# Attention products in quarters of 64 rows by 64 columns, with a second bank for half of the keys

## The chip, the cores and the metric

The kernel runs on one core of a Trainium2 chip. The metric is the device time of one execution in microseconds (us): the median of several runs. A core has five engines that run their own instruction queues in order: TensorE (PE in the profile, its weight loads shown apart as PEld), VectorE (DVE), ScalarE (ACT), GpSimd (POOL) and SyncE (SP, which here only issues DMAs). TensorE's results land in PSUM tiles, of 512 fp32 columns in up to 128 partitions here, called banks below.

## The reference

Two layers over 2708 tokens of 256 channels. Only the attention of the first layer is touched by the change. It has four query heads and two key/value heads of 64 channels, so each key/value head serves two query heads, and it is causal:

```python
q = (h @ wq.T).reshape(Bx, Tx, NH, HD).transpose(0, 2, 1, 3)     # NH = 4, HD = 64
k = (h @ wk.T).reshape(Bx, Tx, NKV, HD).transpose(0, 2, 1, 3)    # NKV = 2
v = (h @ wv.T).reshape(Bx, Tx, NKV, HD).transpose(0, 2, 1, 3)
...
scores = jnp.einsum('bhtd,bhsd->bhts', q, k) / jnp.sqrt(jnp.float32(HD))
scores = jnp.where(causal[None, None], scores, jnp.float32(-1e+30))
att = jax.nn.softmax(scores, axis=-1)
y = jnp.einsum('bhts,bhsd->bhtd', att, v).transpose(0, 2, 1, 3).reshape(Bx, Tx, Cx)
x = x + y @ wo.T
```

Before it comes a graph layer whose softmax is decided by the largest adjacency value of each row; after it comes a mixture of eight experts with two chosen per token (router, gated up and down products). The second layer repeats graph layer and experts with other weights, without attention. All is fp32.

## The kernel before

**Stages.** `first` does the graph part and the attention of layer 0, then come the experts of layer 0 (`experts_blocks`), the graph part of layer 1 (`second`) and the experts of layer 1. The change is all in `first`, which takes the first 470 us or so. Tokens lie in 22 tiles of 128 (the last has 20 rows).

**What runs in `first`.** For each tile, `tile_in` loads the adjacency row block, finds the largest value and its index on DVE (`top`, L994, and `index`, L998), fetches the chosen row by an indirect DMA (`fetch`, L1016), makes q, k and v (L1046) and turns q and k (L1069). For each pair of tiles, `pair(t0)` with t0 = 0, 2, ..., 20 does the attention of those 256 queries against all keys up to them, one block of 128 keys after the other. For a block `sb`:

- `scores` (L1120): for each key/value head g one product of 64 rows (the channels of the head, partitions 64g to 64g + 63) by 128 columns (the keys), streaming 512 columns (two query tiles of two heads). The two g's use the upper and the lower half of the rows of the array and run at the same time. The result is the PSUM tile `stt`, one bank for each g, in two buffers.
- `exps` (L1126): ACT takes the exponential of both banks into the SBUF tile `e`, of which there are four.
- `mask` (L1135): POOL clears what lies above the diagonal, only in the last two blocks.
- `values` (L1146), for two blocks at once: for each g one product of 128 rows (the keys) by 64 columns (the channels of v), which adds into partitions 64g to 64g + 63 of the single PSUM bank `o`. The two g's use the left and the right half of the columns and run at the same time.
- `sums` (L1160, L1165): DVE adds `e` up over the blocks in the single SBUF tile `es`, and so frees `e`.

In the first three pairs (`on_pe`, t0 < 6) the sums are made on PE instead, into the bank `zs` (L1153). When a pair is through, `leave` copies `o` to SBUF (ACT, L1187), `spread` (L1198) sums `es` over partitions by a product with ones, DVE takes the reciprocal (L1203, `turn_over`), POOL multiplies (L1207, `weigh`), PE projects (L1221) and DVE joins the residual (L1225). After the pairs t0 = 4, 10, 16, 18 and 20, `route` makes the router's decision for the tiles that are through: a transposition (L408), logits (L423, into a tile `pg` in the bank `zs`), the choice and the ranks on DVE (L437 to L487, with two products at L467 and L468) and scatters of the rows to the experts on POOL (L1829).

**PSUM.** The stage holds eight banks: two `st` buffers of two banks each, two `mm` banks, one bank `o` and one bank `zs`.

**Who sets the order.** Nothing is scheduled on the fly. Each step is given to `Plan` by `add(engine, length, run, needs, take, give, rank)`; `Plan.issue` plays the steps through with the lengths written there, takes the lowest rank among those that can start, and emits the instructions in that order. So an engine's queue is fixed at build time, and a step that waits holds up all that stands behind it in its queue. Where PE would be idle for over 1 us by the plan and the bank `zs` or `o` is free, `Plan.fill` puts in products that nobody reads (`nobody`, L1287).

**After the last pair.** `early_blocks` runs the first experts' blocks of 128 tokens (L561, L584) in the banks `st`, `zs` and `o` while the last tiles are routed; the experts' stage proper begins after the scatter of the last tiles.

Of the kernel before, what the change touches and what calls it, by code (L numbers as in the profile page):

```python
# [10 lines left out]
F32 = mybir.dt.float32  # L11
AF = mybir.ActivationFunctionType
ALU = mybir.AluOpType
# [4 lines left out]
PE, SP = mybir.EngineType.PE, mybir.EngineType.SP  # L18
PSUM = bass.MemoryType.PSUM

P = 128
# [6 lines left out]
NH, NKV, HD = 4, 2, 64  # L28
# [37 lines left out]
def rows(t):  # L66
    return min(P, N - t * P)
# [6 lines left out]
class Plan:  # L74
# [16 lines left out]
    def add(self, engine, length, run, needs=(), take=(), give=(), rank=0.0, lands=0.0):  # L91
        step = dict(engine=engine, length=length, run=run, needs=[n for n in needs if n is not None],
                    take=take, give=give, rank=rank, lands=lands, end=None)
        self.steps.append(step)
        return step
# [54 lines left out]
def adj_ffn_kernel(ctx, tc, x, adj, vecs, bias_rows, tab, w_gnn0, w_gnn1, wqkv, wo,  # L150
                   r0, r1, w1_0, w3_0, w2_0, w1_1, w3_1, w2_1, out):
    nc = tc.nc
# [655 lines left out]
    def first(X, XB, norms, tops, hd, mb, xs, acc, arena, load_weights):  # L808
# [9 lines left out]
        W2 = NREP * P  # L818
        NQK = (NH + NKV) * HD
        with ExitStack() as s:  # L820
# [5 lines left out]
            afp = s.enter_context(tc.tile_pool(name="afp", bufs=1, space=PSUM))  # L826
            abs_ = s.enter_context(tc.tile_pool(name="abs", bufs=2, space=PSUM))
            qT = ap.tile([P, NT, NREP, P], F32, name="qT")
            kT = ap.tile([P, N], F32, name="kT")
            V = ap.tile([P, NT, NKV * HD], F32, name="V")  # L830
# [4 lines left out]
            for g in range(NKV):  # L835
                for i in range(2):
                    q = 64 * i + 32 * g
# [12 lines left out]
            add = plan.add  # L850
# [3 lines left out]
            for a, b in ((0, 4), (4, NT - 1)):  # L854
                loads.append(add("SP", 0.5, lambda a=a, b=b: nc.sync.dma_start(
                    out=X[:, a:b, :], in_=x[a * P:b * P, :].rearrange("(t p) c -> p t c", p=P)),
                    rank=-9.0, lands=1.5 + 0.4 * (b - a)))
# [22 lines left out]
            a = add("SP", 1.2, load_wq, loads, take=["e"], rank=1.5, lands=3.0)  # L880
# [218 lines left out]
            def pair(t0):  # L1099
# [3 lines left out]
                v = {}  # L1103
                on_pe = t0 < PE_SUMS
                rank = t0 + 2.5
                ready = [made[t0][0], made[t0 + 1][0]]
                end = None

                def c0(sb):
                    return W2 if sb == t0 + 1 else 0  # L1110

                for n in range(0, t0 + 2, 2):
                    two = sbs[n:n + 2]

                    def scores(sb):
                        r = rows(sb)
                        v[sb, "st"] = st = abs_.tile([P, NKV, 2 * W2], F32, tag="st", name="stt")
                        for g in range(NKV):
                            a, b = g * HD, (g + 1) * HD
                            nc.tensor.matmul(st[:r, g, c0(sb):], kT[a:b, sb * P:sb * P + r],  # L1120
                                             qT[a:b, t0 + (sb == t0 + 1):t0 + 2, :, :], start=True, stop=True)

                    def exps(sb):
                        r = rows(sb)
                        v[sb] = e = abe.tile([P, NKV, 2 * W2], F32, tag="e", name="e")
                        nc.scalar.activation(e[:r, :, c0(sb):], v[sb, "st"][:r, :, c0(sb):], AF.Exp,  # L1126
                                             scale=1.0 / HD ** 0.5)

                    def mask(sb):
                        r, e = rows(sb), v[sb]  # L1130
                        if t0 == 0 and c0(sb):
                            nc.gpsimd.memset(e[:r, :, :c0(sb)], 0.0)
                        for g in range(NKV):
                            d = e[:r, g, c0(sb):c0(sb) + W2].rearrange("p (h c) -> p h c", h=NREP)
                            nc.gpsimd.affine_select(out=d, in_=d, compare_op=ALU.is_ge, fill=0.0, base=0,  # L1135
                                                    pattern=[[0, NREP], [1, P]], channel_multiplier=-1)

                    def values(n=n, two=two):
                        if n == 0:
                            v["o"] = afp.tile([P, 2 * W2], F32, tag="o", name="o")  # L1140
                            if on_pe:
                                v["zs"] = afp.tile([P, 2 * W2], F32, tag="zs", name="zs")
                        for i, sb in enumerate(two):
                            r, c = rows(sb), c0(sb)
                            for g in range(NKV):
                                nc.tensor.matmul(v["o"][g * HD:(g + 1) * HD, c:], V[:r, sb, g * HD:(g + 1) * HD],  # L1146
                                                 v[sb][:r, g, c:], start=(n + i == 0), stop=(n + i == t0 + 1))
                        if on_pe:
                            for i, sb in enumerate(two):
                                r, c = rows(sb), c0(sb) if t0 else 0  # L1150
                                for g in range(NKV):
                                    q = 64 * i + 32 * g
                                    nc.tensor.matmul(v["zs"][q:q + 32, c:], allones[:r, :32], v[sb][:r, g, c:],  # L1153
                                                     start=(n == 0), stop=(n == t0))

                    def sums(n=n, two=two):
                        a, b = two
                        if n == 0:
                            v["es"] = ab.tile([P, NKV, 2 * W2], F32, tag="es", name="es", bufs=1)
                            nc.vector.tensor_tensor(v["es"], v[a], v[b], ALU.add)  # L1160
                        else:
                            for sb in two:
                                r, c = rows(sb), c0(sb)
                                es = v["es"][:r, :, c:]
                                nc.vector.tensor_tensor(es, es, v[sb][:r, :, c:], ALU.add)  # L1165

                    es = []
                    for sb in two:
                        a = add("PE", 1.0, lambda f=scores, sb=sb: f(sb), ready, take=["st"], rank=rank)
                        scored[:] = [a]  # L1170
                        b = add("ACT", 1.0, lambda f=exps, sb=sb: f(sb), [a], take=["e"], give=["st"], rank=rank)
                        if sb >= t0:
                            b = add("POOL", 1.6, lambda f=mask, sb=sb: f(sb), [b], rank=rank)
                        es.append(b)
                    last = n == t0
                    if on_pe:
                        end = add("PE", 2.9, values, es + [end], take=["o", "zs"] if n == 0 else [],
                                  give=["e"] * 2, rank=rank)
                        ends = [end]
                    else:  # L1180
                        end = add("PE", 1.9, values, es + [end], take=["o"] if n == 0 else [], rank=rank)
                        ends = [add("DVE", 2.46 if n else 1.25, sums, es + [ends[0] if n else None, end],
                                    take=["es"] if n == 0 else [], give=["e"] * 2, rank=rank)]

                def leave():
                    v["ob"] = ab.tile([P, 2 * W2], F32, tag="osb", name="osb")
                    nc.scalar.copy(v["ob"], v["o"])  # L1187
                    if on_pe:
                        v["zb"] = ab.tile([P, NKV, 2 * W2], F32, tag="es", name="zsb", bufs=1)[:, 0, :]
                        nc.scalar.copy(v["zb"], v["zs"])  # L1190

# [13 lines left out]
                def weigh():  # L1205
                    y = v["yT"].rearrange("p t j c -> p (t j c)")
                    nc.gpsimd.tensor_tensor(out=y, in0=v["ob"], in1=y, op=ALU.mult)  # L1207

                a = add("ACT", 1.2 if on_pe else 0.6, leave, [end], take=["ob", "es"] if on_pe else ["ob"],
                        give=["o", "zs"] if on_pe else ["o"], rank=rank - 1)  # L1210
                a = add("PE", 0.9, spread, [a] + ends, take=["mm"], give=["es"], rank=rank - 1)
                a = add("DVE", 3.4, turn_over, [a], take=["yT"], give=["mm"], rank=rank - 1)
                a = add("POOL", 1.6, weigh, [a], give=["ob"], rank=rank - 1)
                for i in range(2):
                    t = t0 + i
                    r = rows(t)
# [16 lines left out]
                    b = add("PE", 0.9, project_out, [a], take=["mm"], give=["yT"] if i else [], rank=rank - 1)  # L1233
                    b = add("DVE", 0.45, join, [b, made[t][1]], give=["mm"], rank=rank - 1)
                    joined.append(b)
                    b = add("POOL", 1.1, sum_up, [b], rank=rank + 3)
# [2 lines left out]
                g0 = {4: 0, 10: 6, 16: 12, 18: 18, 20: 20}.get(t0)  # L1239
                if g0 is not None:  # L1240
                    sent[t0] = route(add, range(g0, t0 + 2), joined[g0:], summed[g0:] + [folded], cleared, 0, XB, xs[0], af, tr_tile,
                          "mm", lambda: afp.tile([P, 2 * W2], F32, tag="zs", name="pg"), "zs", rank + 3)

            for t in range(0, NT, 2):
                project(t)
# [15 lines left out]
            a = None  # L1261
            weights = []
            for e in range(2):
                a = add("SP", 6.0, lambda e=e: load_weights(e), cleared + [a], rank=NT + 3.0 + e, lands=3.0,
                        take=[] if e else [f"{a}{i}" for i in range(3) for a in ("adj", "low")])
# [1147 lines left out]
```

## Time and profile before

| | us |
|---|---|
| median of 3 runs | 1482.06 (1481.34 to 1487.33) |
| the profiled execution, its own time | 1481.93 |
| its span, first to last instruction | 1479.8 |
| PE busy | 1401.3 (95%) |
| DVE busy | 754.4 (51%) |
| ACT busy | 564.5 (38%) |
| POOL busy | 525.7 (36%) |
| `stt` products (L1120), busy | 132.4 |
| `o` products (L1146), busy | 124.3 |
| mean granted PE clock | 0.984 |

The profile is of one execution; 2.1 us of its time lie outside the span. "Busy" is the union of an engine's instructions in time. An fp32 product appears as two passes, each with its own weight load, so the 264 products at L1120 are 528 records of each kind. A shape such as 64\*128 64x512 is rows times columns of the weights in the array, then partitions and elements that stream. A releaser in brackets is what ended the idle time of the engine before that instruction.

### The profile page before, as it was taken

How to read it: one execution, taken by the hardware profiler on the slowest of the kernel's cores; microseconds unless marked ns; L12 is line 12 of the kernel's file. 1: busy time of each engine (PE TensorE's matmuls, PEld its weight loads, DVE VectorE, ACT ScalarE, POOL GpSimd, SP SyncE). 2: the span in 40 equal slices, each digit the busy share in tenths (PEclk: the TensorE clock that was granted, in tenths of full speed). 3: DMA queues.
4: the chain of work that ended last, by engine and by line, in shares of the span. 5: the costliest groups of instructions: out<-in, count | busy, mean ns of one | idle time of the engine just before them, and what ended most of it. 6: DMA issues, size and time to landing. Idle time of an engine off the chain costs nothing.

```text
span 1479.8 us, 20690 instructions
## 1 busy us (share of the span) xinstructions
PE 1401.3 (95%) x7344; PEld 1021.5 (69%) x7344; DVE 754.4 (51%) x1629; ACT 564.5 (38%) x1123; POOL 525.7 (36%) x677
## 2 busy tenths in 40 slices
PE   6878999999999999999999899999999999999995
PEld 5633433433334887888888878888768878888885
DVE  5688999975676322222222474767665322222221
ACT  2577866755544322222221454444333211222220
POOL 5677668773243312222222210031434212222222
PEclk9999999999999999999999999999999999999998
DMA  7689767440001476575212770624412867553111
GB/s 265 199 296 288 241 208 236 139 146 15 8 30 50 126 218 194 141 195 158 37 16 26 167 154 1 139 66 115 132 58 57 265 171 196 157 161 88 19 18 21
DMA packets 190679, 193.03 MB, mean 130 GB/s; under 512 B 90568, under 2 KB 162728, under 8 KB 187856
## 3 DMA queue, kind: packets, MB, share of 16 engines
q1 hardware_dynamic: 166262, 162.30, 35.5%
q0 software_dynamic: 20032, 25.71, 9.7%
q10 hardware_dynamic: 4270, 3.58, 0.7%
q8 instruction: 60, 0.98, 0.3%
q14 instruction: 55, 0.45, 0.1%
HBM read 119.81 MB, written 56.11 MB: 119 GB/s over the span
## 4 chain that ended last, share of the span: by engine, by line
PE 77%; DVE 8%; DMA 6%; POOL 4%; issue 2%; ACT 2%; another core or an unknown queue 0%; POOLq 0%; DVEq 0%; SPq 0%; ACTq 0%
PE pup L2085 23%; PE po L1602 14%; PE y L2100 12%; PE o L1146 5%; PE stt L1120 4%; DMA X<-hd,ix 3%; PE up L561 3%; PE pup L2116 3%; PE y L2150 1%; DVE es L1165 1%; DVE yT L1203 1%; PE pt L2063 1%; PE pm L1221 1%; PE po L948 1%; PE pt L584 1%
## 5 line engine op out<-in xcount | busy, mean ns | idle before, releaser
L2085 PE MATMUL pup<-xTs,arena 128*128 128x256 f32 (+2 forms) x1320 | 252.3, 350 | 0.6 <-ACT xTs L2068 0.6
L2085 PEld LDWEIGHTS pup<-xTs,arena 128*128 128x128 f32 (+1 forms) x1320 | 219.8, 190 | 27.7 <-PE y L2150 1.5
L1602 PE MATMUL po<-hb,PT 128*128 128x257 f32 (+2 forms) x968 | 226.0, 387 | 2.6 <-DVE PT L1595 2.6
L2089 ACT ACTIVATE sl<-pup 128x256 f32<-128x256 f32 (+1 forms) x210 | 73.7, 351 | 375.1 <-PE pup L2085 354.2
L1602 PEld LDWEIGHTS po<-hb,PT 128*128 128x128 f32 (+2 forms) x968 | 175.9, 188 | 41.6 <-issue 12.7
L2090 DVE TENSOR_TENSOR hT<-sl,pup 128x256 f32<-128x256 f32 (+1 forms) x210 | 79.6, 380 | 228.5 <-ACT sl L2089 228.3
L1126 ACT ACTIVATE e<-stt 128x1024 f32<-128x1024 f32 (+1 forms) x132 | 125.6, 986 | 93.0 <-PE stt L1120 63.8
L621 POOL DMA_INDIRECT out<-ys,XR x44 | 68.0, 1546 | 237.2 <-DVE ys L2103 169.2
L1165 DVE TENSOR_TENSOR es<-es,e 128x1024 f32<-128x1024 f32 x104 | 136.1, 1309 | 29.9 <-ACT e L1126 22.0
L621 POOL DMA_INDIRECT acc<-ys,XR x44 | 68.4, 1554 | 225.1 <-DVE ys L2103 153.7
L2100 PE MATMUL y<-arena,hT 128*128 128x256 f32 x612 | 136.7, 379 | 0.0
L1120 PE MATMUL stt<-qT,kT 64*128 64x512 f32 (+1 forms) x528 | 132.4, 611 | 4.3 <-ACT e L1126 3.9
L1829 POOL DMA_INDIRECT xs<-XR,place x88 | 93.3, 1061 | 91.7 <-DVE mk L1589 39.6
L1146 PE MATMUL o<-e,V 128*64 128x512 f32 (+1 forms) x528 | 124.3, 594 | 0.0
L2100 PEld LDWEIGHTS y<-arena,hT 128*128 128x128 f32 x612 | 114.3, 190 | 14.5
L1580 ACT ACTIVATE E<-sb,dcol 128x768 f32<-128x768 f32 (+1 forms) x88 | 75.3, 859 | 110.2 <-DVE PT L1595 106.7
L2103 DVE TENSOR_SCALAR ys<-y,XR 128x256 f32<-128x256 f32 x71 | 34.3, 484 | 146.6 <-PE y L2100 146.4
L2085 PE MATMUL pup<-xTs,room 128*128 128x256 f32 (+3 forms) x528 | 99.9, 346 | 0.0
L1120 PEld LDWEIGHTS stt<-qT,kT 64*128 64x128 f32 x528 | 44.4, 187 | 76.5 <-issue 62.3
L2085 PEld LDWEIGHTS pup<-xTs,room 128*128 128x128 f32 (+1 forms) x528 | 85.4, 189 | 9.8 <-PE y L2150 0.8
L1146 PEld LDWEIGHTS o<-e,V 128*64 128x64 f32 x528 | 33.0, 138 | 70.6 <-issue 55.6
L994 DVE MAX8 tops<-arena 128x8 f32<-128x2708 f32 (+1 forms) x22 | 65.3, 2970 | 0.3 <-DMA arena<-in_adj 0.3
(316 smaller groups left out, 1992.4 us busy)
## 6 DMA issues: line engine op xcount, KB each, us to landing
more<-in_w SPq DMA_DIRECT2D x48, 640.0 KB
arena<-in_adj SPq DMA_DIRECT2D x21, 1354.0 KB
arena<-in_w SPq DMA_DIRECT2D x36, 640.0 KB
mb<-mb SPq DMA_DIRECT2D x44, 352.0 KB
XR<-xs SPq DMA_DIRECT2D x80, 134.0 KB
xs<-none SPq DMA_DIRECT2D x16, 536.0 KB
room<-in_w SPq DMA_DIRECT2D x12, 640.0 KB
acc<-X SPq DMA_DIRECT2D x21, 128.0 KB
```

The lines of the kernel that those rows point to most:

```text
L621: i = nc.gpsimd.indirect_dma_start(out=acc[:, :], out_offset=bass.IndirectOffsetOnAxis(ap=tokens.bitcast(I32), axis=0), in_=ys, in_offset= ...
L1120: nc.tensor.matmul(st[:r, g, c0(sb):], kT[a:b, sb * P:sb * P + r], qT[a:b, t0 + (sb == t0 + 1):t0 + 2, :, :], start=True, stop=True)
L1126: nc.scalar.activation(e[:r, :, c0(sb):], v[sb, "st"][:r, :, c0(sb):], AF.Exp, scale=1.0 / HD ** 0.5)
L1146: nc.tensor.matmul(v["o"][g * HD:(g + 1) * HD, c:], V[:r, sb, g * HD:(g + 1) * HD], v[sb][:r, g, c:], start=(n + i == 0), stop=(n + i == t ...
L1165: nc.vector.tensor_tensor(es, es, v[sb][:r, :, c:], ALU.add)
L1580: nc.scalar.activation(e[:q, :n], sb[:q, i0:i1], AF.Exp, bias=dcol[:q, j:j + 1], scale=SLOPE - 1.0)
L1602: nc.tensor.matmul(v["po", i][:r, :F], v["PT", j][:q, a:a + r], hb[:q, j, :], start=(j == 0), stop=(j == NT - 1))
L1829: i = nc.gpsimd.indirect_dma_start(out=xs[:, :], out_offset=bass.IndirectOffsetOnAxis(ap=at, axis=0), in_=src, in_offset=None)
L2085: nc.tensor.matmul(pp[:to, i, :B, :], wn[:, c, :], xT[:, c, :B, :], start=(c == 0), stop=(c == KC - 1))
L2089: nc.scalar.activation(sl[:, :B, :], pp[:, 0, :B, :], AF.Silu)
L2090: nc.vector.tensor_tensor(hT[:, n, :B, :], sl[:, :B, :], pp[:, 1, :B, :], ALU.mult)
L2100: nc.tensor.matmul(y, hT[:, n, b, :], w[3][:, n, :], start=(n == 0), stop=(n == NHC - 1))
```

## The change

In the pairs from t0 = 6 on, each score product of 64 rows by 128 columns becomes two of 64 by 64 (keys 0 to 63 and 64 to 127 of the block), and each value product of 128 by 64 becomes two of 64 by 64. The second half of the keys of a value product adds into a bank of its own, `o2`, which takes the place of `zs`. The first three pairs stay as they were. `leave` moves from ACT to DVE in the pairs from t0 = 6 on: a copy of `o` and an addition of `o2`. `route` no longer has a bank for its logits; it uses the `mm` tile of its transposition, which so is held until ACT has copied the logits out (`keep`). The planned length of `values` goes from 1.9 to 1.75.

```diff
+                def keys(sb):
+                    r = rows(sb)
+                    return [(0, r)] if on_pe else [(p, min(p + HD, r)) for p in range(0, r, HD)]
...
                         for g in range(NKV):
                             a, b = g * HD, (g + 1) * HD
-                            nc.tensor.matmul(st[:r, g, c0(sb):], kT[a:b, sb * P:sb * P + r],
-                                             qT[a:b, t0 + (sb == t0 + 1):t0 + 2, :, :], start=True, stop=True)
+                            for p, q in keys(sb):
+                                nc.tensor.matmul(st[p:q, g, c0(sb):], kT[a:b, sb * P + p:sb * P + q],
+                                                 qT[a:b, t0 + (sb == t0 + 1):t0 + 2, :, :], start=True, stop=True)
...
+                            if not on_pe:
+                                v["o2"] = afp.tile([P, 2 * W2], F32, tag="zs", name="o2")
...
-                                nc.tensor.matmul(v["o"][g * HD:(g + 1) * HD, c:], V[:r, sb, g * HD:(g + 1) * HD],
-                                                 v[sb][:r, g, c:], start=(n + i == 0), stop=(n + i == t0 + 1))
+                                for p, q in keys(sb):
+                                    to = v["o2" if p else "o"]
+                                    nc.tensor.matmul(to[g * HD:(g + 1) * HD, c:], V[p:q, sb, g * HD:(g + 1) * HD],
+                                                     v[sb][p:q, g, c:], start=(n + i == 0), stop=(n + i == t0 + 1))
...
-                        end = add("PE", 1.9, values, es + [end], take=["o"] if n == 0 else [], rank=rank)
+                        end = add("PE", 1.75, values, es + [end], take=["o", "zs"] if n == 0 else [], rank=rank)
...
-                    nc.scalar.copy(v["ob"], v["o"])
-                    if on_pe:
+                    if not on_pe:
+                        nc.vector.tensor_copy(v["ob"], v["o"])
+                        nc.vector.tensor_tensor(v["ob"], v["ob"], v["o2"], ALU.add)
+                    else:
+                        nc.scalar.copy(v["ob"], v["o"])
...
-                a = add("ACT", 1.2 if on_pe else 0.6, leave, [end], take=["ob", "es"] if on_pe else ["ob"],
-                        give=["o", "zs"] if on_pe else ["o"], rank=rank - 1)
+                a = add("ACT" if on_pe else "DVE", 1.2, leave, [end], take=["ob", "es"] if on_pe else ["ob"],
+                        give=["o", "zs"], rank=rank - 1)
...
-                          "mm", lambda: afp.tile([P, 2 * W2], F32, tag="zs", name="pg"), "zs", rank + 3)
+                          "mm", None, "mm", rank + 3)
```

## The prediction

> **What bounds the kernel now.** The attention stage ends at about 474 us; what follows is untouched. I read first the forty slices of 37 us in the page, for where which engine is full:
>
> ```profile
> PE   6878999999999999999999899999999999999995
> ...
> DVE  5688999975676322222222474767665322222221
> ```
>
> DVE is at 9 only in slices 5 to 8 (148 to 296 us); PE is at 9 nearly everywhere. So I cut the stage at the starts of `spread` (L1198) and asked for busy times in each stretch. Columns: length, then busy us of PE, PEld, DVE, ACT and POOL with counts, the granted clock, the DMA share and rate:
>
> ```profile
> 252.40:290.00 37.60, 36.41 (x169) 15.93 (x169) 36.05 (x36) 26.47 (x45) 31.70 (x32) 0.95 0.55 168
> 290.00:339.00 49.00, 46.13 (x183) 16.98 (x185) 35.19 (x50) 26.39 (x48) 37.84 (x53) 0.97 0.40 133
> 339.00:379.40 40.40, 39.77 (x178) 14.01 (x176) 24.58 (x20) 21.12 (x33) 9.02 (x11) 1.00 0.02 8
> ```
>
> Two regimes. From 176 to 290 us (pairs 8 to 12) DVE is busy 109.8 of 114 us (36.55 + 37.22 + 36.05 over three stretches): it still finds maxima and indices of adjacency rows. From 290 us on (pairs 14 to 20) PE is the bound, and DVE has 13 to 16 us to spare in each stretch.
>
> Inside the second regime I read PE's weight loads in the timeline (start, us, engine, instruction, idle before it):
>
> ```profile
> 375.45 0.30 PEld L1120 LDWEIGHTS stt<-qT,kT 64*128 64x128 f32 x4 [0.81 <-issue]
> 375.99 0.19 PEld L1120 LDWEIGHTS stt<-qT,kT 64*128 64x128 f32 x2 [0.24 <-issue]
> 376.42 0.19 PEld L1120 LDWEIGHTS stt<-qT,kT 64*128 64x128 f32 x2 [0.23 <-issue]
> 377.37 0.20 PEld L1146 LDWEIGHTS o<-e,V 128*64 128x64 f32 x4 [0.76 <-issue]
> 377.85 0.14 PEld L1146 LDWEIGHTS o<-e,V 128*64 128x64 f32 x2 [0.29 <-ACT e L1126]
> 378.28 0.14 PEld L1146 LDWEIGHTS o<-e,V 128*64 128x64 f32 x2 [0.28 <-issue]
> 378.71 0.14 PEld L1198 LDWEIGHTS pm<-es,allones 128*64 128x64 f32 x2 [0.28 <-issue]
> 379.14 0.14 PEld L1198 LDWEIGHTS pm<-es,allones 128*64 128x64 f32 x2 [0.29 <-issue]
> 380.10 0.73 PEld L1120 LDWEIGHTS stt<-qT,kT 64*128 64x128 f32 x8 [0.81 <-issue]
> ```
>
> A pass of 512 columns takes 0.43 us (375.99 to 376.42), with the next weights loaded while it streams. From `stt` (64\*128) to `o` (128\*64) the next load comes 0.95 us after the last one, not 0.43: the last pass runs out first, about 0.09 us go by, and the first load is exposed. From `o` to L1198, both 128\*64, it comes after 0.43 us as if nothing had changed, though the product differs and its operand comes from DVE. In the chain of waits this gives
>
> ```profile
> 375.52 1.92 PE stt L1120 x8
> 377.44 1.87 PE o L1146 x8
> ```
>
> Four passes are 4 × 0.43 = 1.72 us, so **entering `stt` costs 0.20 us and entering `o` 0.15 us** (its weights are 64 columns, not 128).
>
> [...] 0.15 to 0.20 us between shapes, nothing between equal ones. [...] No row before is 64\*64; nearest are four column tiles in the bank `zs`, in the chain of waits
>
> ```profile
> 98.91 1.00 PE zs L1153 x8
> ```
>
> where two rounds of four cost 2 × 0.43 us and one entry. So I take a block in quarters at two passes, 0.86 us, as now without its entry.
>
> **The change, part by part.** Counts are from the built order of PE's queue, split at the `spread` of pair 12 (290 us before).
>
> 1. *Switches after pair 12.* Before: 31 entries o→stt, 15 stt→o, 20 other→o, 7 other→stt, 27 into other shapes (0.17 each, between the 0.15 of transpositions and the 0.20 of products). 31 × 0.20 + 15 × 0.15 + 20 × 0.15 + 7 × 0.20 + 27 × 0.17 = 17.4 us. After: 28 + 21 changes between o and stt are free; 26 entries from other shapes at 0.15 (64 columns) and 26 into other shapes at 0.17: 8.3 us. **−9.1 us on the engine that bounds.** The doubled instruction count hides under streaming: starts of neighbours in the trace are 7 ns apart, 16 of them 0.11 us of a block's 0.86.
> 2. *Switches before it, pairs 6 to 12:* 10.6 to 8.3 us by the same prices. Counted as 0, because DVE is the bound; worth −2.3 us if it isn't.
> 3. *`leave` on DVE.* The nearest row reads PSUM at this size:
>
> ```profile
> 478.61 0.63 DVE L576 TENSOR_TENSOR chunks<-chunks,up 128x512 f32<-128x512 f32 x1
> ```
>
> I take 0.63 for the copy and 0.63 for the addition, 1.26 us a pair. Four fall in DVE's regime (pairs 6 to 12): +5.0. The built order also moves the last index search (2.97 us) behind pair 12's reciprocal, which takes off 0 to 3.0. I take **+4 us** (2 to 5). What ACT is spared (eight copies of 0.59) is worth nothing: ACT is busy 26 of 49 us.
>
> 4. *Pair boundaries after that.* `leave` stands in DVE's queue ahead of the pair's last two sums (1.23 each), and `spread` waits for those: 0.15 + 1.26 + 2.46 + 0.1 = 4.0 us after the last `o`. PE's cover, two `stt` and two `o` blocks, shrinks to 3.43 us: 0.55 lost. Then the chain that PE waits for does not shrink:
>
> ```profile
> 380.22 3.36 DVE L1203 RECIPROCAL yT<-pm 128x512 f32<-128x512 f32 x1 [5.09 <-PE pm L1198]
> ...
> 383.66 2.11 POOL L1207 TENSOR_TENSOR yT<-osb,yT 128x512 f32<-128x512 f32 x1 [1.38 <-DVE yT L1203]
> ...
> 385.82 1.59 PEld L1221 LDWEIGHTS pm<-wo_sb,yT 128*128 128x128 f32 x8 [2.21 <-POOL yT L1207]
> ```
>
> PE already runs dry here, so the two entries (0.35) saved under it come back as idle time. 0.9 us for each of four boundaries: **+3.6** (1 to 6).
>
> 5. *The router's logits on `mm`.* One more ACT copy for each of eleven turned pairs of tiles (0.26, as for the small L459), beside PE work; an `mm` buffer is held some 1.5 us longer, and there are two. Bound 0 to +3, taken as 0 but for the last pair.
> 6. *The end.* The last pair's chain to the experts is latency: `spread` comes about 1 us later through `leave`, plus one logit copy: **+1.3**. `early_blocks` also waits for `zs` (`leave`, 1.3 us, in place of nothing), which it can spare while the tail runs.
> 7. *Fillers:* 11 of `nobody` after pair 12 vanish, since `zs` is taken. They stood in gaps; no time. If their gaps lower the clock (0.95 to 1.00 here), up to +2.
>
> Sum: −9.1 + 4 + 3.6 + 1.3 = −0.2 on the profiled 1481.93 us, which lies 0.13 under the median: **1482 us**. Its own range, by the bounds of 3 to 7, is 1476 to 1488. A measurement of this kernel can tell about 0.5%, 7.4 us, from no change.
>
> **Rivals.**
>
> *The switches come through (faster).* DVE's regime has slack that I don't see (POOL and the fetches pace it, DVE idle 4 us), so `leave` fits and item 2 counts; boundaries cost 0.3. −9.1 − 2.3 + 1 + 1.2 + 1.3 = −8: 1474 us, at best 1469. For: PE is also at 36.4 of 37.6 us there. Against: 96% busy DVE.
>
> *`leave` becomes the wait (slower).* The next pair's first `o` needs both banks, and both now come free from DVE, whose queue may stand one or two sums back when the last `o` ends. Wait: 1.23 to 2.46 + 1.26 + 0.2 − 1.72 (two `stt` blocks as cover) = 1.0 to 2.2 us. It decides once DVE is over 0.25 us late. At eight pairs 8 to 18 us: 1490 to 1500, middle 1494. For: one bank each, no second buffer, and DVE does run late: at 287 us the sums of a pair come after its `o`. Against: after 339 us DVE is 61 to 73% busy.
>
> *Quarters don't run four at once.* If the halves of the rows took turns, 120 blocks × 2 products × 0.86 = +206 us: 1688. Against: each pair of halves runs together in the rows above.
>
> **How the numbers follow.** No change 0.52, switches come through 0.20, `leave` as wait 0.25, no concurrency 0.03. Nearly all of the first lies within 0.5%; the second is over 0.5% faster in most of its range, the third over 0.5% slower in nearly all. With the edges of the first: faster 0.20, same 0.52, slower 0.28. The range for 8 in 10 takes in most of both neighbours: 1471 to 1495.
>
> **What would show it.** Right: chains of `stt x16` and `o x16` of 1.72 us without exposed loads between them; DVE's copy and addition near 0.63; the `spread` of pair 12 near 294 us, the last `o` within 3 us of 471. Wrong: rows of 64\*64 longer than 0.6 us each (fourth case), `o` waiting for DVE `osb` in the list of waits (third), or pair 12 through by 290 us (second).

## The result, and the profile after

The changed kernel takes **1490.51 us** (median of 17 runs, 1488.05 to 1500.82) where the kernel before takes 1481.66 (17 runs on the same chip): a ratio of **1.0073, 95% interval 1.0059 to 1.0087**. It is slower, by a little more than the half per cent that I had called no change. Below, a ratio is often turned into us by multiplying its distance from 1 by 1481 us; for the change that is +10.8 (8.7 to 12.9), and +8.9 as a difference of medians.

The page of the kernel after, in its forty slices of 37 us:

```profile
PE   6878989988989799999999989999999999999996
DVE  5688999986667422222222474768665322222221
```

PE, which was at 9 in all slices from the fifth to the 22nd, now has five slices of 7 or 8 between the sixth and the fourteenth, and DVE falls off a little later. Busy times between the starts of `spread` (now L1210) of pairs 10, 12, 14, 16, and of pairs 18 and 20, with the columns of the prediction's table (length, busy us and counts of PE, PEld, DVE, ACT, POOL, clock, DMA):

```profile
255.10:295.70 40.60, 38.45 (x301) 16.13 (x298) 38.83 (x43) 31.06 (x50) 29.35 (x33) 1.00 0.62 186
295.70:347.50 51.80, 41.81 (x297) 14.99 (x296) 36.61 (x52) 24.62 (x50) 41.68 (x55) 0.97 0.36 119
347.50:384.20 36.70, 36.04 (x313) 13.05 (x309) 28.72 (x22) 19.75 (x28) 10.79 (x10) 1.00 0.03 8
...
432.60:483.80 51.20, 45.67 (x370) 19.62 (x372) 35.66 (x61) 23.45 (x34) 25.93 (x41) 0.97 0.17 58
```

After pair 12, PE has less to do, as intended: 41.81 us busy in the second row against 46.13 before, 36.04 in the third against 39.77. The third stretch is 3.7 us shorter. But the second is 2.8 us longer although PE does 4.3 us less in it, and the last is 3.4 us longer (51.20 against 47.8). From the `spread` of pair 12 to the start of the last `o`, PE's busy time falls from 174.1 to 163.8 us, and its idle time rises from 6.6 to 17.9. The time saved has turned into idle time.

That the switches are gone shows in PE's weight loads, at a like place in the timeline (start, us, engine, instruction, idle before it):

```profile
376.95 0.15 PEld L1125 LDWEIGHTS stt<-qT,kT 64*64 64x64 f32 x4 [0.28 <-issue]
377.38 0.15 PEld L1125 LDWEIGHTS stt<-qT,kT 64*64 64x64 f32 x4 [0.28 <-issue]
377.81 0.15 PEld L1155 LDWEIGHTS o<-e,V 64*64 64x64 f32 x4 [0.28 <-issue]
```

From `stt` to `o` the next load comes 0.43 us after the last one, as between two loads of `stt`; it was 0.95 before. Each row holds four loads (x4), one for each quarter, so four quarters stream together in the 0.43 us of one pass. In PE's own timeline, a row of two blocks begins 1.72 us after the row before it, with nothing between:

```profile
376.52 1.90 PE L1125 MATMUL stt<-qT,kT 64*64 64x512 f32 x16
378.24 1.90 PE L1155 MATMUL o<-e,V 64*64 64x512 f32 x16
```

And `leave` on DVE, behind pair 12's last `o`, is what I had priced at 0.63 twice:

```profile
290.40 0.66 DVE L1197 COPY osb<-o 128x512 f32<-128x512 f32 x1
291.17 0.69 DVE L1198 TENSOR_TENSOR osb<-osb,o 128x512 f32<-128x512 f32 x1
```

So both prices were nearly right. Where did the time go? I set four marks in the two profiled executions (us):

| | before | after | difference | predicted |
|---|---|---|---|---|
| start to `spread` of pair 12 | 289.9 | 295.7 | +5.8 | +4 |
| from there to the start of the last `o` | 180.7 | 181.7 | +1.0 | −5.5 (items 1 and 4) |
| last `o` to the first product of the experts proper (`pup`) | 37.2 | 43.2 | +6.0 | +1.3 |
| from there to the end | 972.0 | 967.4 | −4.6 | 0 |

The last row can't be put down to the change, which leaves this part of the program as it was: in the fourteen executions profiled here, of as many kernels, it takes 966.6 to 980.2 us. Up to the experts the change costs 12.8 us in these two executions where I had −0.2, and the two larger misses are the second and the third row.

**The third row** can be read in full. PE's timeline after the last `o` (at 470.64) of the kernel before:

```profile
472.19 2.09 PE L561 MATMUL up<-xTs,arena 128*128 128x128 f32 x16 [0.37 <-ACT xTs L546]
474.21 1.08 PE L1198 MATMUL pm<-es,allones 128*64 128x512 f32 x4
...
482.01 2.00 PE L1221 MATMUL pm<-wo_sb,yT 128*128 128x256 f32 x8
483.94 2.86 PE L584 MATMUL pm<-arena,chunks 128*128 128x256 f32 x12
...
489.82 1.03 PE L423 MATMUL pg<-rwn,rT 128*128 128x8 f32 x8
```

And of the kernel after:

```profile
476.87 1.09 PE L1155 MATMUL o<-e,V 64*64 64x512 f32 x8 [0.28 <-ACT e L1131]
479.02 0.91 PE L539 MATMUL pm<-ident,XR 128*128 128x128 f32 x4 [1.06 <-DMA XR<-xs]
479.91 3.88 PE L561 MATMUL up<-xTs,arena 128*128 128x128 f32 x32
483.72 1.08 PE L1210 MATMUL pm<-es,allones 128*64 128x512 f32 x4
484.73 1.59 PE L561 MATMUL rests<-xTs,arena 128*128 128x128 f32 x12
486.16 3.74 PE L561 MATMUL up<-xTs,arena 128*128 128x128 f32 x32
489.73 1.49 PE L561 MATMUL rests<-xTs,arena 128*128 128x128 f32 x12
491.06 2.00 PE L1233 MATMUL pm<-wo_sb,yT 128*128 128x256 f32 x8
492.99 5.45 PE L584 MATMUL pm<-arena,chunks 128*128 128x256 f32 x24
...
501.36 0.96 PE L423 MATMUL pm<-rwn,rT 128*128 128x8 f32 x8
```

Before, the queue had 16 products of `early_blocks` (`up`) ahead of the last `spread`; now it has 32. A second `rests` now stands ahead of the output projection L1233, and 24 products of L584 and 16 `up` stand between that and the router's logits, where there were 12 of L584, a `rests` and a filler. But for 1.06 us in front of the first of them and 0.45 later there is no wait: PE is full, but with work that nobody waits for. `spread` begins 6.4 us after the start of the last `o`, against 3.6 before. The last sums that it needs, which stand behind `leave` in DVE's queue, end 4.6 us after it:

```profile
479.41 2.55 DVE L1174 TENSOR_TENSOR es<-es,e 128x1024 f32<-128x1024 f32 x2
```

So 1.0 us of the delay is what I had forecast for `leave`, and the other 1.8 are products that still stand in front of it. The router's logits (L423) come 24.0 us after the last `o`, against 19.2 before (489.82 less 470.64). Then a second order adds to it, in the chain of waits:

```profile
506.15 1.28 ACT L459
507.43 0.01 issue
507.44 0.22 ACT expo L459
...
509.61 1.02 POOL xs L1841
```

The router's exponential (L459) now stands in ACT's queue behind three evictions of `early_blocks`, and so does the table load of 1.28 us that stands right ahead of it: the last of the evictions ends at 506.13 and the exponential starts at 507.44. The rows can't be scattered (L1841) before their gate is computed from it. From the last `place` (L487) to the first scatter it is 3.10 us (506.51 to 509.61) against 0.96. By steps: +4.8 to the logits, −1.3 from there to `place`, +2.1 to the scatter, +0.4 to `pup`: the 6.0 of the table, but for rounding.

**The second row** has no single wait. PE's waits between 140 and 500 us, in us in total, times, longest:

```profile
PE stt L1125 <- ACT e L1131: 8.2, 8, 2.1
PE pm L1233 <- POOL yT L1219: 6.0, 3, 3.8
PE pm L1069 <- POOL qk L1063: 5.5, 5, 2.4
...
PE o L1155 <- DVE osb L1197: 2.1, 1, 2.1
```

All the first three are also in the list of before, with 3.9, 3.6 and 3.4 us. Such sums don't say by themselves what a wait costs: a kernel below that loses nothing (the bank alone) has 9.2 us of the first. One can be seen at work at the boundary of pairs 18 and 20:

```profile
432.60 1.08 PE L1210 MATMUL pm<-es,allones 128*64 128x512 f32 x4 [0.52 <-DVE es L1174]
433.61 2.49 PE L1125 MATMUL stt<-qT,kT 64*20 64x256 f32 x20
439.94 3.44 PE L1233 MATMUL pm<-wo_sb,yT 128*128 128x256 f32 x8 [3.84 <-POOL yT L1219]
443.31 3.12 PE L1155 MATMUL o<-e,V 64*64 64x512 f32 x24
```

PE stands 3.84 us in front of the projection, with the `o` blocks queued behind it. The projection then takes 3.44 us, not the 2.00 of the same row above: the granted clock is 0.50 from 439.5 to 442.9 us. The trace has three such pieces of 3.4 us (10.2 us) between pair 12 and the last `o`, where before had one. PE was idle through the 3.4 us ahead of this piece; ahead of the other two it was busy for 30 and 42% of them, and ahead of the one of before for 38%. Two more pieces of 3.4 us at half the clock are some 3.4 us lost, by my estimate.

### The profile page after: what moved, and what is told of

Same layout as the page of the kernel before. It is cut to its first block, busy times and chain, and to the rows that moved or that the text cites. A ratio compares the mean times of both kernels' runs of the same rounds, so it can differ in the third digit from the quotient of the medians.

```text
span 1488.0 us, 22463 instructions
## 1 busy us (share of the span) xinstructions
PE 1389.9 (93%) x8238; PEld 1009.0 (68%) x8238; DVE 766.6 (52%) x1645; ACT 561.6 (38%) x1126; POOL 527.0 (35%) x677
## 4 chain that ended last, share of the span: by engine, by line
PE 61%; DMA 1%; DVE 1%; ACT 1%; issue 1%; POOL 0%; POOLq 0%; SPq 0%; ACTq 0%; DVEq 0%
PE pup L2097 23%; PE po L1614 14%; PE y L2112 12%; PE pup L2128 3%; PE up L561 2%; PE y L2162 1%; PE pt L2075 1%; PE pt L584 1%; PE pt L423 1%; PE nobody L1702 1%; PE pn L1513 1%; DMA X<-acc 0%; DMA XR<-xs 0%; DMA arena<-mb 0%; PE pth L2150 0%
## 5 line engine op out<-in xcount | busy, mean ns | idle before, releaser
L1174 DVE TENSOR_TENSOR es<-es,e 128x1024 f32<-128x1024 f32 x104 | 136.1, 1309 | 17.1 <-ACT e L1131 10.1
L1125 PE MATMUL stt<-qT,kT 64*64 64x512 f32 (+1 forms) x1004 | 128.9, 590 | 8.2 <-ACT e L1131 8.2
L1155 PE MATMUL o<-e,V 64*64 64x512 f32 (+1 forms) x1004 | 130.3, 605 | 2.4 <-DVE osb L1197 2.1
L1841 POOL DMA_INDIRECT xs<-XR,place x88 | 92.7, 1054 | 102.3 <-DVE mk L1601 41.0
L1155 PEld LDWEIGHTS o<-e,V 64*64 64x64 f32 (+1 forms) x1004 | 38.7, 138 | 74.0 <-issue 55.2
L1125 PEld LDWEIGHTS stt<-qT,kT 64*64 64x64 f32 (+1 forms) x1004 | 37.3, 137 | 72.3 <-issue 52.1
```

What stands on the lines that cost most here:

```text
L1125: nc.tensor.matmul(st[p:q, g, c0(sb):], kT[a:b, sb * P + p:sb * P + q], qT[a:b, t0 + (sb == t0 + 1):t0 + 2, :, :], start=True, stop=True)
L1155: nc.tensor.matmul(to[g * HD:(g + 1) * HD, c:], V[p:q, sb, g * HD:(g + 1) * HD], v[sb][p:q, g, c:], start=(n + i == 0), stop=(n + i == t0 ...
L1841: i = nc.gpsimd.indirect_dma_start(out=xs[:, :], out_offset=bass.IndirectOffsetOnAxis(ap=at, axis=0), in_=src, in_offset=None)
```

## Experiments

The question is which part costs the time: the quarters, the bank, `leave` on DVE, or the order that the planner makes of them; and in which pairs. In the expectations, theory A is mostly the order, theory B `leave` on DVE, and theory C the bank. Besides the medians I give three marks of each profiled execution: the `spread` of pair 12, from there to the last `o`, and the tail from the last `o` to `pup`. Before they are 289.9, 180.7 and 37.2, after 295.7, 181.7 and 43.2. A profiled execution lies up to 5.6 us from the median of its kernel, so the first two marks can be several us off; the tail, which is one chain, repeats better.

**The planned length of the scores.** The planner takes 1.0 us for a block of scores, and the trace has 0.86. If the order is bad because its lengths are untrue, a truer length should mend it.

```diff
-  a = add("PE", 1.0, lambda f=scores, sb=sb: f(sb), ready, take=["st"], rank=rank)
+  a = add("PE", 1.0 if on_pe else 0.87, lambda f=scores, sb=sb: f(sb), ready, take=["st"], rank=rank)
```

> The changed kernel with one number altered: the planned length of a score step is 0.87 in place of 1.0 in the pairs from t0 = 6 on (what a block in quarters measures). The queues' order is planned anew with it; no operation is added or removed. Theory A, the loss is an order planned with lengths that no longer hold: within 4 us of 1480, and the wait of 3.8 us before the output projection near 440 us shrinks. Theory B, the loss is the evacuation on VectorE, and theory C, it is the bank taken from the router: within 3 us of the changed kernel (1490).

Measured: 1518.41 us, ratio 1.0234 (1.0209 to 1.0259). But for six more passes of fillers, no instruction differs from the kernel after except in its place, and it is slower than that kernel by 24 us by the ratios and 28 by the medians; in the profiled executions 20.4 us of it lie ahead of `pup`. Half clock takes 27 us between pair 12 and the last `o`. The idea that a truer length gives a better order fell. What remains is that order alone can move this stage by some 20 us, more than any price in my sum.

**`leave` on ACT, the addition on POOL.**

```diff
-  nc.vector.tensor_copy(v["ob"], v["o"])
-  nc.vector.tensor_tensor(v["ob"], v["ob"], v["o2"], ALU.add)
+  nc.scalar.copy(v["ob"], v["o"])
+  nc.scalar.copy(v["ob2"], v["o2"])
...
+  whole = [] if on_pe else [add("POOL", 1.3, both_halves, [a], give=["ob2"], rank=rank - 1)]
```

> The changed kernel, but the two banks o and o2 are copied to SBUF by ScalarE (two copies of 0.59 us), and GpSimd adds the second copy to the first while VectorE still makes the reciprocal. VectorE has no part in leave any more; quarters and banks are as in the changed kernel. Theory B (leave on VectorE costs the time): 1478 +- 4. Theory A (order): the order changes too, but by chance, within 4 us of 1490. Theory C (bank): within 3 us of 1490.

Measured: 1495.49 us, ratio 1.0095 (1.0075 to 1.0115); marks 296.8, 188.5, 36.8. The tail is as short as before, though `leave` is planned at 1.2 us here too, so it is tied to `leave` on DVE. The rest is worse than in the kernel after, and the trace doesn't lay it to POOL: the projection's wait for POOL is 3.7 us (6.0 after), and that of L1069 for POOL's `qk` is 0.6 (5.5). What has grown is the wait of `stt` for ACT's exponentials, 13.2 us in ten times (8.2 in eight), and half clock (20.5 us between pair 12 and the last `o`). That ACT's two copies a pair bring this about is not shown.

**The bank alone.** The kernel before, where pairs from 6 on hold `zs` as well without using it, and the router's logits go to `mm`.

```diff
-  end = add("PE", 1.9, values, es + [end], take=["o"] if n == 0 else [], rank=rank)
+  end = add("PE", 1.9, values, es + [end], take=["o", "zs"] if n == 0 else [], rank=rank)
...
-                        "mm", lambda: afp.tile([P, 2 * W2], F32, tag="zs", name="pg"), "zs", rank + 3)
+                        "mm", None, "mm", rank + 3)
```

> The kernel before with one part of the change alone: the pairs from t0 = 6 on hold the bank zs from their first value product to their leave although nothing is written to it, and the router's logits go to the mm tile of their transposition. Products, shapes and leave are as before. Theory C (bank): +6 to +10 us against before. Theories A and B: within 3 us of before.

Measured: 1482.40 us, ratio 1.0004 (0.9991 to 1.0016); marks 291.8, 177.8, 36.3. The bank, the router on `mm` and the missing fillers (6 `nobody` passes are left of 60 between 140 and 480 us) cost nothing that shows.

**`leave` on DVE alone, with two readings.** The kernel before; DVE copies `o` twice, in place of the copy and the addition; planned 1.2.

```diff
-  nc.scalar.copy(v["ob"], v["o"])
+  nc.vector.tensor_copy(v["ob"], v["o"])
+  nc.vector.tensor_copy(v["ob"], v["o"])
```

> The kernel before with one part of the change alone: leave of the pairs from t0 = 6 on is on VectorE, as two readings of the bank o (the copy made twice), planned at 1.2. Shapes and banks are as before. Theory B: +6 to +12 us against before, more in 176 to 350 us, where VectorE is full. Theory C: within 3 us. Theory A: +2 to +5 us, what VectorE's regime loses.

Measured: 1500.33 us, ratio 1.0125 (1.0109 to 1.0140), marks 296.8, 181.4, 41.9. Without a single quarter it is slower than the kernel after: 18.5 us, for eight times 1.3 us on DVE. And its tail has the order of the kernel after. PE's timeline, behind the last `o` (at 478.28):

```profile
479.70 3.87 PE L561 MATMUL up<-xTs,arena 128*128 128x128 f32 x32 [0.24 <-ACT xTs L546]
483.50 1.08 PE L1201 MATMUL pm<-es,allones 128*64 128x512 f32 x4
...
492.78 5.45 PE L584 MATMUL pm<-arena,chunks 128*128 128x256 f32 x24
...
501.14 0.96 PE L423 MATMUL pg<-rwn,rT 128*128 128x8 f32 x8
```

Again 32 `up` products ahead of `spread` and 24 of L584 ahead of the logits. So it is `leave` on DVE, planned at 1.2 us, that lets the planner put the others first; it needs no quarters for that.

**`leave` on ACT, no addition.** The kernel after, where ACT copies `o` and `o2` is left out of the result, so that the change gives DVE nothing to do; planned 0.6.

```diff
-  nc.vector.tensor_copy(v["ob"], v["o"])
-  nc.vector.tensor_tensor(v["ob"], v["ob"], v["o2"], ALU.add)
+  nc.scalar.copy(v["ob"], v["o"])
```

> The changed kernel, but leave is on ScalarE as in the kernel before and copies the bank o alone; it leaves out the addition of o2, so the second half of the keys of each block is missing from the output. Quarters, both banks and the router's logits on mm are as in the changed kernel. Theory B (the quarters are worth 9 us, leave on VectorE costs more than that): 1472 +- 4. Theory A (any order that the planner makes with wrong lengths loses by chance): 1484 to 1496.

Measured: 1484.90 us, ratio 1.0027 (1.0015 to 1.0040); marks 290.8, 187.8, 36.2. The tail is back to 36 us, with quarters in the last pair, but there is still no gain. DVE's work is therefore not all of it: the stretch from pair 12 to pair 14 is 56.7 us (49.0 before), although DVE has nothing more to do. Half clock takes 17.1 us between pair 12 and the last `o` (3.4 before).

**The quarters where PE is the bound, but for the last pair.** Quarters, `o2` and `leave` on DVE for pairs 14, 16 and 18 only.

```diff
+  quarters = 14 <= t0 < 20
...
-  return [(0, r)] if on_pe else [(p, min(p + HD, r)) for p in range(0, r, HD)]
+  return [(p, min(p + HD, r)) for p in range(0, r, HD)] if quarters else [(0, r)]
```

> Quarters, o2 and leave on VectorE only in the pairs t0 = 14, 16 and 18, which lie in TensorE's regime; pairs 6 to 12 and the last pair 20 are as in the kernel before (router's logits on mm throughout, which cost nothing by itself). Theory B: pair 12 is through by 292 us as before, and the three pairs bring 5 to 7 us: 1476 +- 4. Theory A: within 3 us of 1490 or anywhere above before.

Measured: 1478.36 us, ratio 0.9984 (0.9973 to 0.9996); marks 289.2, 177.0, 36.1. Here the change gains, 2.4 us (0.6 to 4.0), less than the 5 to 7 expected. The tail is as before: 16 `up` products ahead of `spread`, and the logits 18.9 us after the last `o`.

**With the last pair.** The same, with `quarters = 14 <= t0`.

> As the kernel with quarters in pairs 14 to 18, and in the last pair 20 as well. Theory B with a dear tail (the last leave on VectorE delays the router of the last tiles): 2 to 5 us above that kernel, in the stretch from the last o to the first product of the experts' stage. If the tail costs what the prediction said (1.3 us), the last pair's own gain of 2 us outweighs it: the same or 1 us below.

Measured: 1486.34 us, ratio 1.0035 (1.0020 to 1.0049); marks 292.2, 176.7, 42.3. One pair more turns a gain of 2.4 us into a loss of 5.2: **the last pair costs 7.6 us** (some 4.8 to 10.3, from the two intervals). From pair 12 to the last `o` it loses nothing (176.7 against 177.0), and the tail has the order seen twice:

```profile
470.66 3.87 PE L561 MATMUL up<-xTs,arena 128*128 128x128 f32 x32
474.46 1.08 PE L1213 MATMUL pm<-es,allones 128*64 128x512 f32 x4
...
492.11 0.96 PE L423 MATMUL pm<-rwn,rT 128*128 128x8 f32 x8
```

The logits come 23.2 us after the last `o`. Here PE waits for the DMA of the first `early_blocks` only 0.28 us, so the 1.06 us of the kernel after are not what makes the tail long.

**`leave` on DVE alone, with one reading.** The kernel before, with one copy of `o` on DVE, planned 0.6.

> The kernel before with leave of the pairs from t0 = 6 on moved to VectorE as a single copy (planned at 0.6, as on ScalarE): half of VectorE's work of the experiment with two readings, which cost 19 us. If VectorE's busy time is the price: +6 to +11 us. If it is the place in VectorE's queue (a step that waits for TensorE ahead of the sums and of the index searches): +14 to +20, nearly all of it. Theory A: anywhere from 0 to +20.

Measured: 1487.88 us, ratio 1.0044 (1.0030 to 1.0058); marks 303.6, 178.4, 36.7. One reading, planned at 0.6, leaves the tail alone, and costs 6.5 us in the pairs before; with two it was 18.5. That the second reading costs 12 us is more than its tail of some 5 us explains. In the one profiled execution with two readings, 8.2 us of the loss lie behind `pup` (980.2 us to the end, 972.0 before), where the change touches nothing; why, I can't say.

**The quarters in pairs 6 to 12 alone**, with `leave` on DVE there (`quarters = 6 <= t0 < 14`).

> Quarters, o2 and the leave on VectorE for pairs 6 to 12 alone; pairs 14 to 20 as before; router logits on mm. Theory A (what costs is the order that the planner makes of VectorE's regime: the last search for indices falls behind pair 12's reciprocal, as in after): 1486 to 1492 us, last FIND_INDEX8 at 310 us or later, pair 12 at 294 to 297, and the stretch from pair 12 to pair 14 over 52 us. Rival B (four leaves of 1.3 us on VectorE and nothing else): pair 12 at 294, the stretch from 12 to 14 as before (49), 1485 to 1487. Rival C (the early pairs cost nothing, the whole loss is the last pair's tail): 1479 to 1483.

Measured: 1484.17 us, ratio 1.0029 (1.0018 to 1.0041), that is 4.3 us (2.7 to 6.1); marks 290.7, 182.0, 36.1. The last search for indices starts at 307.3 us (289.9 before). Rival C is out. Theory A had it somewhat dearer than it is and pair 12 later; rival B had the right size. Where the time goes can't be read from this trace: its execution is the fastest of the 22, 3.6 us under their median, and no slower than before. The stretch from pair 12 to 14 is 51.7 us in it against 49.0, with DVE as busy as before (35.54 against 35.19 us).

The two parts add up: 4.3 of pairs 6 to 12 and 5.2 of pairs 14 to 20 are 9.5, and the change as a whole has 10.8 (8.7 to 12.9).

**The same without the addition.** ACT copies `o`, planned 0.6; the half of the keys in `o2` is left out of the result.

> As the quarters for pairs 6 to 12 alone, but the leave stays one ScalarE copy of o, and the lower half of the rows (o2) is left out of the result; VectorE gets no work at all from the change, while its order is still the new one (last search for indices behind pair 12's reciprocal). Theory A (order): still 1484 to 1488 us, with the search after 310 us and the stretch from 12 to 14 over 52 us. Rival B (VectorE's time): 1479 to 1482 us, pair 12 at 290 or earlier.

Measured: 1487.31 us, ratio 1.0046 (1.0026 to 1.0066), 6.8 us; marks 288.3, 187.2, 36.0, the search at 311.4. Rival B is out: with nothing more on DVE the early pairs cost no less, and the stretch from pair 12 to 14 is 53.3 us in an execution close to the median. That leaves the order, or the quarters in these pairs themselves: no kernel here has the quarters in the order of before, so the order is argued by exclusion and not shown.

**A split `leave` in pairs 14 to 20.** ACT copies `o`; DVE adds `o2` with one reading; `spread` waits for the copy alone, and the weighing for both.

```diff
-  a = add("DVE" if quarters else "ACT", 1.2 if on_pe or quarters else 0.6, leave, [end], ...)
+  a = add("ACT", 1.2 if on_pe else 0.6, leave, [end], ...)
+  whole = [add("DVE", 0.66, second_half, [a], give=["zs"], rank=rank - 1)] if quarters else []
...
-  a = add("POOL", 1.6, weigh, [a], give=["ob"], rank=rank - 1)
+  a = add("POOL", 1.6, weigh, [a] + whole, give=["ob"], rank=rank - 1)
```

> Quarters for pairs 14 to 20; the leave is split: ScalarE copies o, VectorE adds o2 with one reading (planned 0.6 and 0.66), and only the weighing waits for the addition, so that spread waits for the copy alone. Theory A (the last pair's loss is that spread waits for VectorE's two readings and is put behind all 32 up passes): from the last o to the first expert product 36 to 37.5 us as before, 1475 to 1479 us. Rival (the last pair's quarters hold zs and o longer, so early_blocks and the tail are late whoever does the leave): over 40 us from the last o on, 1484 to 1488.

Measured: **1476.60 us, ratio 0.9972 (0.9959 to 0.9986)**; marks 293.5, 174.4, 39.9. It beats both kernels, by 4.1 us against before and, in medians, by 14 against the kernel after. Against the same quarters with two readings on DVE it is 9.3 us less (0.9972 against 1.0035). The tail, at 39.9, is not all the way back: PE's queue still has a few `early_blocks` more ahead of the router, PE waits 1.05 us for a DMA ahead of them, and the logits come 21.1 us after the last `o`. The kernel below has the same order there, and a tail of 37.7.

**A split `leave` in all pairs from 6 on.**

> Quarters for all pairs from 6, as in the change, with the split leave. Theory A (order of VectorE's regime costs 4 to 6 us, the later pairs give 4 to 6 back, the tail is as before): 1480 to 1485 us, last FIND_INDEX8 after 310 us. Rival B (VectorE's time: one reading of 0.65 us a pair in place of two): 1476 to 1480 us with pair 12 at 292 and the stretch from 12 to 14 below 47.

Measured: 1479.02 us, ratio 0.9994 (0.9983 to 1.0004); marks 289.4, 180.3, 37.7, the search at 307.2. It is the change as it stands but for `leave`: 0.9994 against 1.0073, some 12 us. And it is 0.0022 above the kernel that leaves the early pairs alone, 3.3 us (some 0.8 to 5.8, from the two intervals): the early quarters cost something whatever engine takes `leave` (3.3 split, 4.3 on DVE, 6.8 on ACT, with intervals that overlap). Which move of the order costs that is open. The late search for indices is common to all of them, but the kernel with two readings and no quarters has it too (312.8), with a stretch from pair 12 to 14 of 47.6 us. And that stretch, long in all others with early quarters (51.7 to 60.9 us), is not long here: 49.1, in an execution 3.1 us under the median.

## Why the prediction was wrong

The median forecast was no change; it became slower by 0.59 to 0.87%. The time lies inside the range given. The range that the bounds of items 3 to 7 make is 1477 to 1490 when they are added up, not 1476 to 1488. Of the signs named, the rows of 1.72 us and the lengths of `leave` came; the last `o`, put within 3 us of 471, began at 477.4.

**The step that failed is item 6, the end:** +1.3 us was put on it, and the tail became 6.0 us longer; by the medians, the last pair as a whole costs 7.6. What it left out is the order of the queues behind the last pair, as told below.

- **The switches (item 1): right in PE's work.** Entries between `stt` and `o` cost nothing that shows any more (0.43 us from load to load). PE's busy time from pair 12 to the last `o` fell by 10.3 us; 3.3 of these are the fillers that are gone, and half clock, three pieces against one, works the other way, so −9.1 is of the right size. The prices of 0.15 to 0.20 us an entry, read in the trace of before, carried this step rightly. In time, some 4 of these 9 us came through: with the split `leave`, pairs 14 to 20 gain 4.1 us (2.1 to 6.1). That items 1, 4 and 6 add up to −4.2 for these pairs is chance: 4 and 6 are prices of `leave` on DVE, and with `leave` on DVE the same pairs lose 5.2.
- **Quarters concurrent: right,** at 0.43 us for four. That the two halves of the keys need a bank each is not shown: no run adds both into one.
- **The pairs in DVE's regime (items 2 and 3): right size, wrong cause.** I had +4, and the quarters of pairs 6 to 12 cost 4.3. But I had it as DVE's own time, and the kernel without DVE's work shows no less. So the agreement in size is luck. The move of the index search that I had seen in the order, and had entered as a gain of up to 3 us, goes with a loss.
- **The pair boundaries (item 4):** in the two kernels with quarters from pair 14 on, the stretch from pair 12 to the last `o` is shorter by 4.0 and 6.3 us, where items 1 and 4 together had −5.5. This is no more than a hint, since the kernel with the bank alone has a stretch shorter by 2.9 in its one execution. In the kernel after it is longer by 1.0, since the early pairs' order and two more windows of half clock fall in it.
- **The router on `mm` and the fillers (items 5 and 7): right.** Together with the bank, 0.6 us (−1.3 to 2.4). Half clock was not their doing: it stayed low in the kernel with the bank alone, which has as few fillers (granted clock 1.00 from 291.8 to 469.6 us).
- **The end (item 6): this step failed.** "`spread` comes about 1 us later through `leave`" took the rest of the queue as it was. `leave` itself did cost that 1 us. The planner, told of 1.2 us on DVE, put another 16 `up` products in the time (it does not with ACT at 1.2 or DVE at 0.6), and with that shifted the projection, the logits and the router's exponential.
- **The rivals.** The slower one had 1494 us by the wait of the next pair's first `o` for both banks. That wait occurs once, for 2.1 us. The outcome was on its side, the mechanism was another: the wait became one of order, in the last pair. My sentence on `early_blocks` ("which it can spare while the tail runs") looked at whether `early_blocks` could wait, and not at who would wait for `early_blocks`.

My working counted the built order of PE's queue for the pairs, and not for the 40 us behind the last one, where the order of PE's and ACT's queues decides.

## What to carry to other kernels

Where an order is fixed at build time by planned lengths, a step moved to another engine changes not only its own time but which work is put ahead of it: compare the built queues up to the end of the stage, and first where a chain of small steps ends it. Time saved on the bound engine came through best here where the step that collects the results doesn't hold the next link of the chain: let the chain wait for one half, and do the rest beside it. Try a change in the pairs where its engine is the bound before it is given to all.

## What the runs showed of the hardware

Four 64 by 64 quarters, two of which add into one bank and two into another, stream at the rate of one pass: four loads every 0.43 us, back to back over two different products. From `stt` to `o`, both in quarters, the next load comes 0.43 us after the last one, as within one product; with the 64\*128 and 128\*64 of before it was 0.95.

A halved clock followed idle time of 1.96 us. In the kernel after, PE is busy for 1.44 of 3.40 us here, and then the clock is halved for the next 3.4 (columns as above):

```profile
388.30:391.70 3.40, 1.44 (x16) 0.86 (x9) 3.27 (x3) 1.85 (x2) 2.11 (x1) 1.00 0.00 0
391.70:395.10 3.40, 3.40 (x14) 1.82 (x16) 2.37 (x5) 1.10 (x5) 1.32 (x2) 0.50 0.09 32
```

From pair 12 to 14, the kernel with the shorter planned length has one wait of PE of 5.6 us, the next longest in its list being 2.5; the clock of that stretch is 0.86 on average:

```profile
301.70:362.60 60.90, 50.23 (x321) 18.20 (x323) 38.95 (x53) 29.81 (x57) 48.68 (x63) 0.86 0.37 115
```

The missing 14% of 60.9 us are at most some 8.5 us by my estimate, which no wait names: the halved clock may have cost this stretch more than its longest wait. Three kernels are far longer than before from pair 12 to the last `o`: `leave` on ACT without the addition, `leave` on ACT with POOL, and the planned length, by 7.1, 7.8 and 14.2 us. Half clock takes 17.1, 20.5 and 27.3 us in them against 3.4 before, and half of what that is more is 7, 9 and 12 us (my estimate, from one execution each). But it isn't the clock alone: pairs 6 to 12 without the addition are 6.5 us longer there with 6.8 us of half clock.
